# Maxima and denominators by way of DRAM, exp four steps behind, and another rule for handing out the pieces: a stack of four cross-attention layers

## Chip, cores and metric

The kernel runs on one core of a Trainium2 chip. The metric is the device time of one execution in microseconds (us); the time before is the median of three runs, 5645.32 us. The engines are named as the profile names them: PE is TensorE (PEld its weight loads), DVE is VectorE, ACT is ScalarE, POOL is GpSimd, SP is SyncE, whose queue issues most DMAs.

## What is computed

Four cross-attention layers one after another on x of 2048 rows by 256, with a context of 1601 rows by 512 and float32 throughout. Layers 0, 2 and 3 ("masked" in the kernel) have 16 heads of 64; a few columns of the logits get a bias of -20 where a mask says so. Layer 1 ("grouped") normalizes x first and has 16 heads of 16 that share 4 key heads. Cut to what matters:

```python
def masked_layer(h, ctx, Wq, Wk, Wv, Wo, bo, ...):
    q, k, v = h @ Wq, ctx @ Wk, ctx @ Wv                     # 16 heads of 64
    logits = einsum('bhqd,bhkd->bhqk', q, k) * 64 ** -0.5
    logits = logits + col_bias                               # -20 in up to four token columns
    out = einsum('bhqk,bhkd->bhqd', softmax(logits), v)
    return h + out @ Wo + bo

def grouped_layer(x, ctx, wq, wk, wv, wo, norm_w):
    q = rmsnorm(x, norm_w) @ wq                              # 16 heads of 16, 4 key heads
    attn = softmax(einsum('btgrd,bsgd->bgrts', q, ctx @ wk) * 0.25)
    return x + einsum('bgrts,bsgd->btgrd', attn, ctx @ wv) @ wo
```

The softmax is computed with its true row maxima, in two passes over the scores.

## The kernel before

**Blocks, units, steps.** A block is a pair of heads in a masked layer (8 blocks of 4 units: four groups of 512 query rows), or one key head with its four query heads in the grouped layer (4 blocks of 8 units: four groups of rows by two pairs of heads). That makes 128 units, 96 masked and 32 grouped. A unit works with two heads and 512 rows; its 1601 keys are cut into `NT` = 13 chunks of 128 (the last has 65). The main loop at the end of the function runs over steps. In one step TensorE computes the scores of chunk `ca` of unit `ka`, and the exp of another chunk `cb` and the product with the values of a third, `cv`, both of the unit before or the one before that, are done: exp follows the scores by 13 + `DELAY` steps and the values follow exp by `LAG` = 1. "Step 4" of a unit means `ca` = 4 below.

**A masked unit.** Scores go to a PSUM tile `s` (two buffers of two banks each). ACT copies them to SBUF as `p` (L763; a pool `probs` of `NP` = 17 buffers), DVE keeps the running maximum `top` over the chunks (L766, L768). After the last chunk, at step 0 of the next unit, `maxima` turns `top` by eight transposes (L805) and reduces it to `ntop`, the negated maximum of each query row (L806). At step 1 `maxima_spread` brings these values to all partitions with eight more transposes (L818) into the PSUM tile `less`. From step 2 on, DVE adds `less` to `p` (L834), ACT takes exp (L841), and POOL adds the chunks up in `sums` (L844 adds the first two, L846 each further one). TensorE multiplies by the values into `po` (L869), and ACT copies the result to `oT` (L875).

**The end of a unit** goes by pieces: `denominators` turns `sums` by eight transposes (L888), reduces them to one denominator per row (L889) and takes the reciprocal; POOL spreads the two columns over 64 rows each (`by`, L899); `divide` turns `by` with four transposes (L907) and DVE multiplies it with `oT` (L911); `project` multiplies by `Wo` (L917, two pieces) and DVE adds the result to `xs`, the running x (L923). A grouped unit has its denominators as a row of `oT` (L894) and then goes the same way; its scores are computed twice, once for the maxima and once, with the maxima subtracted inside TensorE, for exp.

**The queue of pieces.** What is neither scores nor values is handed out in pieces, mostly one at the end of a step: two query pieces for the next unit (five or three in the grouped layer, with the stacking of split operands), the pieces that end a unit, and the projections of the next block's keys (13 pieces) and values (13). They come in groups; a group that has begun is finished first, then groups in `urgent` go before those in `fill`. `Pieces.step(share)` adds a share to a credit and runs one piece for each whole credit. The share is at least 1, and steps 0 and 1 of a masked unit get none. At step 0 of each unit, before its scores, `flush` runs the group that has begun and everything urgent. Nearly all pieces (not the masked denominators) use the one-bank PSUM tile `pm`, which has one buffer.

**Order.** A loop at the end of the program ties the instructions of TensorE, ACT and DVE to the order in which they are written. POOL's and SP's are ordered by the framework's scheduler.

**Loads.** The transposed context lies in DRAM (`ctxT`); slices of it (`ct`, three buffers) are loaded when the group before the one that uses them begins. `wk` and `wv` have two buffers.

## Time and profile before

| | |
|---|---|
| runs | 5645.32 us median of 3 (5644.31 to 5645.62) |
| profiled execution | 5653.54 us, of it 5651.8 in the span of the profile |
| busy | PE 94%, DVE 71%, ACT 57%, POOL 50% of the span |
| mean granted TensorE clock | 0.980 |
| stages | masked layer 0 to about 1534 us, grouped layer to about 2829, masked layers 2 and 3 to the end |
| PE busy, 170 to 1000 us | 793.79 of 830.00 |
| PE busy, 1534 to 2829 us | 1250.58 of 1295.00 |
| PE busy, 4241 to 5390 us | 1104.34 of 1149.00 |
| costliest group of PE | L869 `po<-p,v`: 1821.7 us |
| costliest group of POOL | L846 `sums<-sums,p`: 2499.2 us, 2367 ns each |
| HBM | 235.27 MB read, 13.76 MB written |

The profile is one execution. "Busy" of PE counts matmuls whose ends are modelled and which are pipelined, so two that follow each other overlap a little in its rows; what one costs is better read from the start of one to the start of the next. In a row such as "PE s L751 <- DVE top L768: 116.4, 71, 2.7" the engine, tile and line that waited stand first, then what it waited for, the total in us, the number of times and the longest. A granted clock of 0.5 means that TensorE got half its pulses.

### The profile page before, as it was taken

How to read it: one execution, taken by the hardware profiler on the slowest of the kernel's cores; microseconds unless marked ns; L12 is line 12 of the kernel's file. 1: busy time of each engine (PE TensorE's matmuls, PEld its weight loads, DVE VectorE, ACT ScalarE, POOL GpSimd, SP SyncE). 2: the span in 40 equal slices, each digit the busy share in tenths (PEclk: the TensorE clock that was granted, in tenths of full speed). 3: DMA queues.
4: the chain of work that ended last, by engine and by line, in shares of the span. 5: the costliest groups of instructions: out<-in, count | busy, mean ns of one | idle time of the engine just before them, and what ended most of it. 6: DMA issues, size and time to landing. Idle time of an engine off the chain costs nothing.

```text
span 5651.8 us, 59516 instructions
## 1 busy us (share of the span) xinstructions
PE 5321.4 (94%) x22444; PEld 1865.2 (33%) x22444; DVE 4013.6 (71%) x4140; ACT 3196.2 (57%) x3513; POOL 2837.7 (50%) x1380
## 2 busy tenths in 40 slices
PE   6999999998889999999999999999999999999997
PEld 3333333332323333233233333333333333333332
DVE  3777777777765555555567777777777777777786
ACT  2666666665433434333456666666666666666665
POOL 1766666665410000000056666666666666666676
PEclk8999999999889999999999999999999999999998
DMA  4112211111100000001012111212111121111100
GB/s 135 32 57 60 59 49 53 55 56 44 39 20 5 9 9 9 9 13 52 15 51 61 56 54 49 57 56 59 46 56 55 54 59 49 53 56 52 54 17 15
DMA packets 209744, 252.88 MB, mean 45 GB/s; under 512 B 43529, under 2 KB 155401, under 8 KB 209456
## 3 DMA queue, kind: packets, MB, share of 16 engines
q1 hardware_dynamic: 206192, 243.69, 14.8%
q8 instruction: 177, 2.90, 0.2%
q0 software_dynamic: 1152, 3.28, 0.2%
q10 hardware_dynamic: 2112, 2.10, 0.1%
q14 instruction: 111, 0.91, 0.1%
HBM read 235.27 MB, written 13.76 MB: 44 GB/s over the span
## 4 chain that ended last, share of the span: by engine, by line
PE 78%; ACT 7%; POOL 7%; DVE 5%; issue 2%; DMA 0%; SPq 0%; ACTq 0%; POOLq 0%; DVEq 0%
PE po L869 24%; PE s L751 20%; PE pm L384 6%; PE pm L369 5%; PE pm L917 5%; POOL sums L844 4%; ACT p L763 4%; ACT p L841 3%; POOL sums L846 3%; PE s L850 2%; PE s L784 2%; PE pm L420 2%; PE s L805 2%; PE b L818 2%; PE s L855 2%
## 5 line engine op out<-in xcount | busy, mean ns | idle before, releaser
L846 POOL TENSOR_TENSOR sums<-sums,p 128x1024 f32<-128x1024 f32 (+1 forms) x1056 | 2499.2, 2367 | 1097.9 <-ACT p L841 1084.8
L763 ACT COPY p<-s 128x1024 f32<-128x1024 f32 (+1 forms) x1248 | 1263.4, 1012 | 1434.0 <-PE s L751 1138.3
L869 PE MATMUL po<-p,v 128*64 128x512 f32 (+1 forms) x6656 | 1821.7, 626 | 36.5 <-ACT p L841 34.7
L768 DVE TENSOR_TENSOR top<-s,top 128x1024 f32<-128x1024 f32 (+1 forms) x1056 | 1291.5, 1223 | 753.9 <-ACT p L763 749.4
L751 PE MATMUL s<-q,kT 64*128 64x512 f32 (+1 forms) x4992 | 1426.3, 648 | 117.6 <-DVE top L768 116.4
L834 DVE TENSOR_TENSOR p<-p,b 128x1024 f32<-128x1024 f32 (+1 forms) x1248 | 1504.7, 1206 | 2.4 <-PE b L818 2.0
L841 ACT ACTIVATE p<-p 128x1024 f32<-128x1024 f32 (+1 forms) x1248 | 1321.5, 1059 | 110.3 <-DVE p L834 109.4
L869 PEld LDWEIGHTS po<-p,v 128*64 128x64 f32 (+1 forms) x6656 | 332.0, 136 | 1032.1 <-issue 698.9
L899 POOL COPY by<-rden 128x512 f32<-128x512 f32 x128 | 78.5, 613 | 1111.8 <-DVE rden L897 1083.9
L751 PEld LDWEIGHTS s<-q,kT 64*128 64x128 f32 (+1 forms) x4992 | 370.7, 182 | 732.7 <-issue 454.6
L859 ACT ACTIVATE p<-s 128x1024 f32<-128x1024 f32 (+1 forms) x283 | 289.8, 1024 | 451.0 <-PE s L855 450.9
L844 POOL TENSOR_TENSOR sums<-p 128x1024 f32<-128x1024 f32 x96 | 226.5, 2360 | 434.2 <-ACT p L841 434.2
L789 DVE TENSOR_REDUCE row_top<-s 128x2 f32<-128x1024 f32 x261 | 318.6, 1221 | 122.9 <-PE s L784 121.9
L384 PEld LDWEIGHTS pm<-wv,ct 128*128 128x128 f32 (+1 forms) x2392 | 284.7, 187 | 218.9 <-issue 215.9
L384 PE MATMUL pm<-wv,ct 128*128 128x128 f32 (+1 forms) x2392 | 337.6, 286 | 0.5 <-ACT v L389 0.5
L369 PE MATMUL pm<-ct,wk 128*128 128x512 f32 (+1 forms) x736 | 315.8, 544 | 2.7 <-ACT kT L374 2.7
L917 PE MATMUL pm<-o,wo 128*128 128x512 f32 x512 | 292.0, 653 | 7.1 <-DVE xs L923 2.9
L859 ACT ACTIVATE p<-b 128x1024 f32<-128x1024 f32 (+1 forms) x133 | 136.2, 1024 | 217.8 <-PE b L855 217.8
L923 DVE TENSOR_TENSOR xs<-pm,xs 128x512 f32<-128x512 f32 x232 | 158.4, 683 | 90.4 <-PE pm L917 90.4
L806 DVE TENSOR_REDUCE ntop<-s 128x8 f32<-128x1024 f32 x96 | 117.6, 1225 | 130.9 <-PE s L805 130.6
L789 DVE TENSOR_REDUCE row_top<-b 128x2 f32<-128x1024 f32 x123 | 150.2, 1221 | 62.2 <-PE b L784 61.6
L420 PE MATMUL pm<-xT,wq 128*128 128x512 f32 x336 | 188.5, 644 | 0.0
(191 smaller groups left out, 3279.2 us busy)
## 6 DMA issues: line engine op xcount, KB each, us to landing
ct<-ctxT SPq DMA_DIRECT2D x288, 512.0 KB, 3.8
xT<-xT SPq DMA_DIRECT2D x104, 512.0 KB, 3.5
ct<-ctxT SPq DMA_DIRECT2D x48, 130.0 KB, 2.6
wk<-in_L_xattn_Wk_dram SPq DMA_DIRECT2D x24, 256.0 KB, 4.4
wv<-in_L_xattn_Wv_dram SPq DMA_DIRECT2D x24, 256.0 KB, 3.1
xT<-xs SPq DMA_DIRECT2D x12, 512.0 KB, 2.6
wq<-in_L_xattn_Wq_dram SPq DMA_DIRECT2D x24, 128.0 KB, 2.1
wo<-in_L_xattn_Wo_dram SPq DMA_DIRECT2D x24, 128.0 KB, 2.1
```

Of the source, the lines that this page charges most:

```text
L369: nc.tensor.matmul(u.pk[:, :n], u.wk[:, k, :], ct(k, a, n), start=(k == 0), stop=(k == NCT - 1),)
L384: nc.tensor.matmul(u.pv[:m, c - c0, :], ct(k, a, m), u.wv[:, k, :], start=(k == 0), stop=(k == NCT - 1),)
L751: nc.tensor.matmul(s[:m, h, :], self.u.kT[r, a : a + m], self.q[r, :], start=True, stop=(a != TAIL),)
L763: nc.scalar.copy(p[:m], s[:m])
L768: nc.vector.tensor_tensor(self.top[:m], s[:m], self.top[:m], ALU.max)
L789: nc.vector.tensor_reduce(self.top[:, :, q, k : k + 1], s, AX.X, ALU.max)
L834: nc.vector.tensor_tensor(self.p[c][:m], self.p[c][:m], self.less[:m], ALU.add)
L841: nc.scalar.activation(p[:m], p[:m], AF.Exp)
L844: nc.gpsimd.tensor_tensor(self.sums, self.p[0], p, ALU.add)
L846: nc.gpsimd.tensor_tensor(self.sums[:m], self.sums[:m], p[:m], ALU.add)
L869: nc.tensor.matmul(self.po[r, :], u.v[:m, c, r], self.p[c][:m, h, :], start=(c == 0), stop=(c == NT - 1),)
L917: nc.tensor.matmul(py, wo[:, ts(k, P)], self.o, start=True, stop=True)
```

## The change

- **Maxima.** `maxima` writes `ntop` to DRAM (1024 values, four at a time) and reads it back into an SBUF tile `spread` on all 128 partitions (512 KB moved), both by SP's queue; `maxima_spread`, now at step 3, is one ACT copy from `spread` into the PSUM tile `less`. L818's transposes go. `DELAY` is 4, and `probs` has 19 buffers.
- **Denominators.** They are taken one head at a time (four transposes into `pm`, a reduce), each counted as half a piece; the reciprocals go the same way by DRAM to a tile `by`, and POOL multiplies `oT` with it in place. L899, L907 and L911 go.
- **Sums.** POOL begins `sums` with a copy of the first chunk.
- **Queue.** A piece returns its cost (1.0 if it returns nothing; `divide`, `keep`, `squares` and the four divisions of `normalize` 0.0). The credit carries at most 0.9 over; the share is what is left divided by the steps left, without a floor of 1, with 5 pieces planned for each further unit of the block. Only step 0 after a masked unit gets none. Queries become due at step 3, denominators at step 6, divide and project at step 11.
- **Loads.** Each `ct` load is issued after the piece that last read the buffer, three at the start of a block. `wk` and `wv` have one buffer.

The diff's core:

```diff
...
     masked_names = ["L0_xattn_", "L2_xattn_", "L3_xattn_"]
-    NP = 17
+    NP = 19
     const = ctx.enter_context(tc.tile_pool(name="const", bufs=1))
...
             u.kT = u.v = None
             u.wq = weights.tile([P, NC, P], FP, name="wq")
-            u.wk = weights.tile([P, NCT, P], FP, name="wk")
-            u.wv = weights.tile([P, NCT, P], FP, name="wv")
+            u.wk = weights.tile([P, NCT, P], FP, name="wk", bufs=1)
+            u.wv = weights.tile([P, NCT, P], FP, name="wv", bufs=1)
             for to, w in ((u.wq, "Wq"), (u.wk, "Wk"), (u.wv, "Wv")):
...
             )
+    def on_all_partitions(cols, to):
+        rows = dram.tile([2, P, QT], FP, name="cols", bufs=4)
+        with nc.allow_non_contiguous_dma(reason="1024 values, four at a time"):
+            nc.sync.dma_start(out=rows.rearrange("h p q -> p h q"), in_=cols)
+        for tile_, heads_ in to:
+            src = rows[heads_].rearrange("(o h) p q -> o (h p q)", o=1)
+            nc.sync.dma_start(out=tile_, in_=src.to_broadcast(tile_.shape))
...
                         nc.tensor.transpose(pt[:, h, q, :], self.top[:, h, ts(q, P)], ident)
                 nc.vector.tensor_reduce(ntop, pt, AX.X, ALU.max, negate=True)
+                self.spread = work.tile([P, 2, P, QT], FP, name="spread", bufs=1)
+                on_all_partitions(
+                    ntop, [(self.spread.rearrange("n h p q -> n (h p q)"), slice(0, 2))]
+                )
             else:
...
             if self.masked:
                 self.less = ps_b.tile([P, 2, QB], FP, name="b")
-                for h in range(2):
-                    for q in range(QT):
-                        nc.tensor.transpose(
-                            self.less[:, h, ts(q, P)],
-                            self.ntop[:, h, q : q + 1].to_broadcast((P, P)), ident,
-                        )
+                nc.scalar.copy(
+                    self.less.rearrange("n h (q p) -> n h q p", p=P),
+                    self.spread.rearrange("n h p q -> n h q p"),
+                )
                 return
...
                 p = self.p[c]
                 nc.scalar.activation(p[:m], p[:m], AF.Exp)
-                if c == 1:
+                if c == 0:
                     self.sums = work.tile([P, 2, QB], FP, name="sums")
-                    nc.gpsimd.tensor_tensor(self.sums, self.p[0], p, ALU.add)
-                elif c:
+                    nc.gpsimd.tensor_copy(self.sums, p)
+                else:
                     nc.gpsimd.tensor_tensor(self.sums[:m], self.sums[:m], p[:m], ALU.add)
...
             return self.sub == len(self.layer.SUBS) - 1
-        def denominators(self):
-            rden = self.rden = small.tile([P, 2, QT], FP, name="rden")
+        def denominators(self, h):
+            if h == 0:
+                self.rden = small.tile([P, 2, QT], FP, name="rden")
+            rden = self.rden
             if self.masked:
-                pt = ps_s.tile([P, 2, QT, P], FP, name="s")
-                for h in range(2):
-                    for q in range(QT):
-                        nc.tensor.transpose(pt[:, h, q, :], self.sums[:, h, ts(q, P)], ident)
-                nc.vector.tensor_reduce(rden, pt, AX.X, ALU.add)
+                pt = ps_m.tile([P, QT, P], FP, name="pm")
+                for q in range(QT):
+                    nc.tensor.transpose(pt[:, q, :], self.sums[:, h, ts(q, P)], ident)
+                nc.vector.tensor_reduce(rden[:, h, :], pt, AX.X, ALU.add)
+                if h == 0:
+                    return 0.5
                 nc.vector.reciprocal(rden, rden)
...
                     )
                 nc.vector.reciprocal(rden, pd.rearrange("p q h -> p h q"))
-            self.by = work.tile([P, QT, 2, 64], FP, name="by", bufs=1)
-            nc.gpsimd.tensor_copy(
-                self.by,
-                rden.rearrange("p h (q o) -> p q h o", o=1).to_broadcast((P, QT, 2, 64)),
+            by = work.tile([P, P, QT], FP, name="by", bufs=1)
+            on_all_partitions(
+                rden,
+                [(by[self.rows(h)].rearrange("r p q -> r (p q)"), slice(h, h + 1)) for h in range(2)],
             )
+            self.by = by.rearrange("r p q -> r q p")
+            return 0.5 if self.masked else 1.0
+        def denominator_groups(self):
+            return [[lambda h=h: self.denominators(h)] for h in range(2 if self.masked else 1)]
         def divide(self):
-            pr = ps_m.tile([P, QB], FP, name="pm")
-            for q in range(QT):
-                nc.tensor.transpose(
-                    pr[:, ts(q, P)], self.by[:, q].rearrange("p h o -> p (h o)"), ident
-                )
-            self.o = work.tile([P, QB], FP, name="o", bufs=1)
-            nc.vector.tensor_tensor(self.o, pr, self.oT, ALU.mult)
+            oT = self.oT.rearrange("r (q p) -> r q p", p=P)
+            nc.gpsimd.tensor_tensor(oT, oT, self.by, ALU.mult)
+            return 0.0
         def project(self, k):
             py = ps_m.tile([P, QB], FP, name="pm")
             wo = self.layer.wo(self.u, self.sub)
-            nc.tensor.matmul(py, wo[:, ts(k, P)], self.o, start=True, stop=True)
+            nc.tensor.matmul(py, wo[:, ts(k, P)], self.oT, start=True, stop=True)
             to = xs[:, self.b, k, :]
...
         def finish_groups(self):
-            return [[self.denominators], [self.divide]] + [
-                [lambda k=k: self.project(k)] for k in range(NC)
-            ]
+            return [[self.divide]] + [[lambda k=k: self.project(k)] for k in range(NC)]
...
                 queue = self.urgent or self.fill
                 if not queue:
-                    return
+                    return 1.0
                 self.now.extend(queue.popleft())
-            self.now.popleft()()
+            cost = self.now.popleft()()
+            return 1.0 if cost is None else cost
         def step(self, share):
-            self.credit = min(self.credit + share, 2.0)
+            self.credit = min(self.credit, 0.9) + share
             while self.credit >= 1.0:
-                self.pop()
-                self.credit -= 1.0
+                self.credit -= self.pop()
...
         layer = layers[l]
         nxt = made[l, n] = layer.load(n)
-        slices = {}
-        ahead = deque()
-        def load(name):
-            if name in ahead:
-                ahead.remove(name)
-                kind, c, a, width = name
-                slices[kind, c] = context_slice(a, width)
+        slices, loads = {}, deque()
         def with_loads(queue):
             found = []
             for name, group in queue:
                 if name:
-                    ahead.append(name)
-                def head(name=name, piece=group[0]):
-                    load(name)
-                    if name and ahead:
-                        load(ahead[0])
-                    piece()
-                found.append([head, *group[1:]])
+                    kind, c, a, width = name
+                    slices[kind, c], tiles = context_slice(a, width)
+                    loads.extend(tiles)
+                    each = len(group) // len(tiles)
+                    def read(j, piece, each=each):
+                        piece()
+                        if (j + 1) % each == 0 and loads:
+                            loads.popleft()()
+                    group = [lambda j=j, piece=piece, r=read: r(j, piece) for j, piece in enumerate(group)]
+                found.append(list(group))
             return found
         first, second = map(with_loads, layer.key_groups(nxt, slices))
+        for _ in range(min(3, len(loads))):
+            loads.popleft()()
...
         return normalize(l + 1, b)
-    DELAY, LAG = 2, 1
+    DELAY, LAG = 4, 1
     N = len(units) * NT
+    due = {}
     turn = 0
-    for step in range(N + NT + DELAY + LAG):
+    for step in range(N + NT + DELAY + LAG + 10):
         ka, ca = divmod(step, NT)
...
                 pieces.flush(pieces.fill, pieces.later)
                 start_block(i)
+        top = of[ka - 1] if 0 < ka <= len(units) and ca < DELAY else None
         three = not (scoring and scoring.masked) and not (exping and exping.masked)
...
         if valuing:
             valuing.values(cv)
-        if top and ca == 1:
+        if top and ca == DELAY - 1:
             top.maxima_spread()
         if scoring and ca == 2 and ka + 1 < len(units):
             ahead = unit_of(ka + 1)
-            pieces.urgent.extend(ahead.layer.unit_groups(ahead))
+            due.setdefault(step + 1, []).extend(ahead.layer.unit_groups(ahead))
         if valuing and cv == NT - 1:
-            pieces.urgent.extend(valuing.finish_groups())
-            pieces.urgent.extend(after(kv))
+            due.setdefault(step + 2, []).extend(valuing.denominator_groups())
+            due.setdefault(step + 7, []).extend(valuing.finish_groups() + after(kv))
+        pieces.urgent.extend(due.pop(step, ()))
         if scoring and ca == 4 and units[ka - 1][:1] == units[ka][:1] != units[ka - 2][:1]:
             pieces.fill.extend(pieces.later)
             pieces.later.clear()
-        if scoring and not (top and top.masked):
+        if scoring and not (top and top.masked and ca == 0):
             i, b, sub = units[ka]
             after_this = sum(u[0] == i for u in units[ka + 1 : ka + 8])
-            steps = NT - ca + (NT - 2) * after_this
-            pieces.step(max(1.0, (pieces.left() + 6 * after_this) / steps))
+            steps = NT - ca + (NT - 1) * after_this
+            pieces.step((pieces.left() + 5 * after_this) / steps)
         elif not scoring:
...
```

More of the change, by code (lines that the diff above doesn't have):

```diff
@@ L200, in context_slice, with load @@
         step = NCT if n <= 256 else NCT // 2
-        tiles = []
-        for k in range(0, NCT, step):
-            ct = work.tile([P, step, 2 * QB // step], FP, name="ct", bufs=3)
+        tiles = {}
+        def load(k):
+            tiles[k] = ct = work.tile([P, step, 2 * QB // step], FP, name="ct", bufs=3)
             nc.sync.dma_start(out=ct[:, :, :n], in_=ctxT_dram[:, k : k + step, a : a + n])
-            tiles.append(ct)
-        return lambda k, b, m: tiles[k // step][:, k % step, b - a : b - a + m]
+        loads = [lambda k=k: load(k) for k in range(0, NCT, step)]
+        return lambda k, b, m: tiles[k - k % step][:, k % step, b - a : b - a + m], loads
     def first_context_slice(i):
@@ L482, in load @@
                         nc.gpsimd.tensor_copy(self.last_k[:, g, to], ident[:, j : j + 16])
-                self.wk = weights.tile([P, NCT, 2, 64], FP, name="wk")
-                self.wv = weights.tile([P, NCT, 64], FP, name="wv")
+                self.wk = weights.tile([P, NCT, 2, 64], FP, name="wk", bufs=1)
+                self.wv = weights.tile([P, NCT, 64], FP, name="wv", bufs=1)
                 for half in range(2):
@@ L674, in squares @@
             nc.scalar.activation(held["x"], xs[:, b], AF.Square)
+            return 0.0
         def rms():
@@ L696, in divide @@
                 nc.sync.dma_start(out=xT_dram[l][b], in_=held["x"])
+            return 0.0
         return [[squares], [rms], *([lambda q=q: divide(q)] for q in range(QT))]
@@ L897, in denominators @@
                 nc.vector.reciprocal(rden, pd.rearrange("p q h -> p h q"))
-            self.by = work.tile([P, QT, 2, 64], FP, name="by", bufs=1)
-            nc.gpsimd.tensor_copy(
-                self.by,
-                rden.rearrange("p h (q o) -> p q h o", o=1).to_broadcast((P, QT, 2, 64)),
-            )
+            by = work.tile([P, P, QT], FP, name="by", bufs=1)
+            on_all_partitions(
+                rden,
+                [(by[self.rows(h)].rearrange("r p q -> r (p q)"), slice(h, h + 1)) for h in range(2)],
+            )
+            self.by = by.rearrange("r p q -> r q p")
+            return 0.5 if self.masked else 1.0
+        def denominator_groups(self):
+            return [[lambda h=h: self.denominators(h)] for h in range(2 if self.masked else 1)]
         def divide(self):
-            pr = ps_m.tile([P, QB], FP, name="pm")
-            for q in range(QT):
-                nc.tensor.transpose(
-                    pr[:, ts(q, P)], self.by[:, q].rearrange("p h o -> p (h o)"), ident
-                )
-            self.o = work.tile([P, QB], FP, name="o", bufs=1)
-            nc.vector.tensor_tensor(self.o, pr, self.oT, ALU.mult)
+            oT = self.oT.rearrange("r (q p) -> r q p", p=P)
+            nc.gpsimd.tensor_tensor(oT, oT, self.by, ALU.mult)
+            return 0.0
         def project(self, k):
@@ L1087, in spare @@
             return ps_s.tile([P, 2, QB], FP, name="s")
-        top = of[ka - 1] if ka and ca < 2 and ka - 1 < len(units) else None
         if step == 3:
```

## The prediction

> **What bounds the kernel now.** I read the busy row first, then the waits of TensorE, then the timeline of one quiet stretch of the masked layers, then two places where the timeline is not quiet.
>
> ```profile
> PE 5321.4 (94%) x22444; PEld 1865.2 (33%) x22444; DVE 4013.6 (71%) x4140; ACT 3196.2 (57%) x3513; POOL 2837.7 (50%) x1380
> ```
>
> The timeline's columns are start, duration, engine, line, operation, tiles; in brackets the idle time before it and its releaser.
>
> ```profile
> 3528.58 1.13 PE L751 MATMUL s<-q,kT 64*128 64x512 f32 x4
> ...
> 3529.64 1.08 PE L869 MATMUL po<-p,v 128*64 128x512 f32 x4
> ...
> 3530.65 1.12 PE L369 MATMUL pm<-ct,wk 128*128 128x512 f32 x2
> ...
> 3530.86 1.22 DVE L768 TENSOR_TENSOR top<-s,top 128x1024 f32<-128x1024 f32 x1 [0.77 <-ACT p L763]
> ...
> 3531.71 1.13 PE L751 MATMUL s<-q,kT 64*128 64x512 f32 x4
> ```
>
> A step is scores 1.06, values 1.01, one queue piece 1.06 (start to start): 3.13 us of TensorE without a hole. Per step ACT has 1.01+1.06, DVE 1.21+1.22, POOL 2.37. So TensorE sets the pace: work taken from it is won, and any hole in it is lost. Its present holes:
>
> ```profile
> PE s L751 <- DVE top L768: 116.4, 71, 2.7
> PE pm L907 <- POOL by L899: 55.9, 79, 4.4
> ```
>
> The first starts at ACT's copy L763 of step 4, which waits for POOL's first sum L844 to free a probability buffer. Grouped layer: 1250.6 us of TensorE in the 1295 us from 1534 to 2829, a step without a piece taking 2.30 (2118.03 to 2120.33). It is TensorE's too.
>
> **What is removed.** L818: eight transposes, 1.02 a unit in the chain of waits, 96 masked units: 98 us. L907: four, 0.55 start to start, 128 units: 70. The hole at L751: POOL's copy frees the first buffer after about 1.2 (twice the 0.61 of the 128x512 copy L899) instead of after the second exp and 2.36, and 19 buffers with four steps' delay leave the same two steps: 116. Next in line there is step 4's exp, a whole step ahead of its values. The hole at L907: 56. Sum 340. DVE loses L911 (88 us) and gains some 17 by two reduces of 0.7 for one of 1.22; it had room, so nothing.
>
> **Maxima by DRAM.** Seen from the start of scores at step 0, ntop is ready at 3.4 (3499.84 to 3503.26). The DMAs: a write of 4 KB in 16-byte pieces, then a 512 KB broadcast in 4 KB rows.
>
> ```profile
> xT<-xT SPq DMA_DIRECT2D x104, 512.0 KB, 3.5
> ...
> wq<-in_L_xattn_Wq_dram SPq DMA_DIRECT2D x24, 128.0 KB, 2.1
> ...
> wo<-in_L_xattn_wo_dram SPq DMA_DIRECT2D x16, 16.0 KB, 1.7
> ...
> tok_idx<-ttn_token_indices_A_dram SPq DMA_DIRECT2D x3, 1.0 KB, 3.2
> ```
>
> The write lies between 1.7 (near in amount) and 3.2 (near in piece size); I take 2.2. The broadcast is like xT, 3.5. It lands at 9.2, at worst 10.3; ACT wants it 3.3 into step 3, at 11.6 to 12.6. Hidden, with 1.3 us left; each us past that costs up to 96. SP holds weights, context and xT loads too, but the trace shows them issued out of written order (wq at 3424.97, its wv at 3500.50), so I let none stand in front. ACT's copy is 96 times about 1.01 (L763), beside TensorE where step 3 has a piece. Where it has none, ACT has 5.7 us for two steps of 5.2, and the next values wait for exp and the oT copy: about 1.0, in half the units: 48.
> The Trainium skill, "DMA: Bandwidth & Descriptors" (Specifications), says that transfers under 512 B are read and rewritten, which speaks against 16-byte writes. No row here prices such a write; the bounds above do without it.
>
> **The queue.** This decides. I stepped the new rule through all steps (share, cost, due step). Pieces that follow each other with no scores between them share the one ps_m bank, and TensorE must wait for the evacuation, which DVE does after that step's maximum. The old kernel has such a pair once:
>
> ```profile
> 2847.64 1.12 PE L917 MATMUL pm<-o,wo 128*128 128x512 f32 x2
> ...
> 2849.46 0.68 DVE L923 TENSOR_TENSOR xs<-pm,xs 128x512 f32<-128x512 f32 x1
> ...
> 2850.19 1.12 PE L917 MATMUL pm<-o,wo 128*128 128x512 f32 x2 [1.43 <-DVE xs L923]
> ```
>
> New pairs in masked units: (a) project(0) and project(1), due at step 11, come together there, or the second is flushed at step 0 just after the first: 86 times. In the quiet frame project ends at 3.13, the maximum at 3.50, the evacuation at 4.2: 1.1 each, 95 us. (b) Both halves of the denominators in one step, since after the first 0.5 the credit is still over 1 (example: shares 0.95, credit 1.58): 64 times. Transposes end at 2.58, reduce at 4.2: 1.67 each, 107. About 30 stand apart and cost DVE's lag, 0.5 each: 15. (c) A last key piece flushed ahead of project waits 0.7 for ACT: 21 times, 15. (d) Steps without a piece wait about 0.1 for exp, one a unit: 10. With ACT's 48: 290.
>
> In grouped blocks the rule plans 5 a unit where about 7 come (queries 3 or 5, denominators 1, projections 2) and key pieces besides. Example, the second grouped block's second unit: 14 pieces left over 82 steps plus 5 for each of 6 units gives a share of 0.54; the five query pieces, due at step 3, take until step 11, and the denominators are left for the flush at step 0, where divide and project follow them at once. TensorE then stands for the whole round trip: DVE 0.6, write 2.2 with its issue, second broadcast 0.4 + 2.1 (wq's row), POOL's multiply 1.2 (half of 2.37): 6.5. In 11 units nothing lies between: 72. In 4, one step of 2.3: 4.2 each, 17. In 14, two steps: 1.9 each, 27. Some 30 pairs of project with project or a stack wait 0.85 (2112.57 to 2113.38): 26. Sum 142.
>
> A hole also slows what follows:
>
> ```profile
> 1478.12 0.58 PE L529 MATMUL pm<-q,sel_qa 128*128 128x512 bf16 x1 [2.61 <-DVE q L536]
> ...
> 1478.64 2.31 PE L751 MATMUL s<-q,kT 64*128 64x512 f32 x4
> ```
>
> Scores took 2.31, not 1.13; the window 1474 to 1482 has a granted clock of 0.79. In the quiet frame 3.4 us at half rate lose 1.7. I give that to the 15 long holes and a third of it to the 14 short: 35. The holes of 1.7 in masked units were there before (71 at L751), so nothing for them.
> The Trainium skill, "TensorE: Matmul & The Clock Gate" (What's actually happening), has half rate follow only an idle window of about 3.4 us. The 2.61 here is less and slowed it all the same; by the rule alone, with nothing for the 14 short holes, the sum would be 9 lower.
>
> **Rest.** Between layers the normalize pieces, spaced a step apart before, come in one bunch in three units (cost 0.0 each): four reciprocals (0.95) with two products (0.61) hold DVE 8.7 us in one go. Between 0 and 50; I take 25. The last block has few pieces, and divide comes one or two steps after the denominators; with the final round trip through DRAM: 15. Single wk and wv buffers cost nothing: wk's last reader is half a block before its next use, and wv is loaded while keys are projected; context loads stay three tiles ahead. If that cover failed, one load of 3.1 to 4.4 a block would show, 28 blocks, 120.
>
> POOL gains 128 multiplies of 1.2 and loses 128 copies of 0.61: about 31 of 40 us a unit. Divide needs no written place on POOL: three to five steps pass between denominators and project in masked units, and POOL waits 0.76 a step.
>
> Sum on the profiled execution's own 5653.5 (span 5651.8 and 1.7 around it): -340 +290 +142 +35 +25 +15 = 5820. The median is 8 below the profiled one: 5812. Between 5645 and this stand 167 us.
>
> **Rivals.** Faster: pairs don't meet. If the evacuation of the first of a pair is done earlier than my frame has it, or the credit spaces them, the 202 us of (a) and (b) are not paid: 5610. It decides once 167 of the 507 us added fail to come. For it: TensorE alone would have 40.1 us a masked unit (busy 166.8 of the 174.0 from 3545 to 3719, four units, less 1.57 each) against 43.5 now. Against: the 1.43 shown, a plain consequence of one bank.
> Slower, divide on POOL stands behind that step's sum: in the frame the sum runs from 3.34 to 5.71 and divide to 6.9, with project waiting since 2.07: 4.8 in 96 units: 6270; half of it, 6040. For it: before, L907 does wait for POOL 79 times. Against: POOL is free between sums.
> Slower, the broadcast lands 2 us late: ACT stops, 96 x 2: 6000. Against: xT's worst landing of 5.2 still comes within 0.5 us.
> The change doesn't free the buffer, the L751 hole staying: 5930.
>
> **Numbers.** Forecast 0.63, pairs apart 0.22 (a tenth of it within 0.2% of no change), POOL order 0.06, late broadcast 0.05, buffer 0.04. Low 5600 leaves out half of that rival, high 5960 the POOL case and part of the late one: under 0.2 together. The forecast's own range is 5700 to 5900: the bunch 0 to 50, the write 1.7 to 3.2, pairs 0.8 to 1.7. About 0.2% (11 us) is what a measurement can tell from no change: faster 0.2, same 0.02, slower 0.78.
>
> **What would show it.** Right: no L818 or L907; the L751 wait for DVE's top nearly gone; TensorE at project waiting for xs and for POOL's divide, some 70 us of the latter in 1534 to 2829; the second half of the denominators waiting for rden; grouped units about 45 us for 40; masked units 43 to 44; more half-clock windows in the grouped layer. Wrong: masked units near 41, grouped units at or below 40, or ACT's less copy waiting on a DMA.

## The result and the profile after

The changed kernel takes 5969.71 us (median of four runs, 5964.33 to 5977.5) against 5644.82 of the kernel before beside it: ratio 1.0577, interval 1.0559 to 1.0596. It is slower, as forecast, but by 325 us instead of 167, 10 us above the range of 5600 to 5960. The profiled execution has a span of 5964.1, 312.3 longer than before. From here on line numbers are those of each kernel's own file; in the changed kernel scores are L766, values L886, project L938.

The busy row of the page shows TensorE 67 us less busy and a lower share of a longer span: the loss is holes and, as shown below, slower matmuls behind them, not added work.

```profile
PE 5254.2 (88%) x21064; PEld 1731.4 (29%) x21164; DVE 3947.2 (66%) x4108; ACT 3370.5 (57%) x3609; POOL 3053.7 (51%) x1476
```

The waits of TensorE name the holes (total us, times, longest):

```profile
PE pm L938 <- POOL oT L931: 209.1, 52, 9.2
PE po L886 <- ACT oT L892: 117.3, 94, 4.1
PE pm L906 <- DVE rden L907: 91.0, 64, 1.6
PE pm L938 <- DVE xs L944: 87.2, 100, 3.5
PE po L886 <- ACT p L858: 40.4, 28, 8.1
PE pm L938 <- ACT kT L376: 16.1, 21, 0.8
```

The 116.4 of scores waiting for the running maximum is gone. Two rows stand here with the forecast's very counts, 64 meetings of the two halves of the denominators and 21 of a key piece with project; the meetings at `xs` on this row are 100: 81 in masked units, where 86 were forecast, and 19 in the grouped layer, where some 30 were. The two largest rows are larger than forecast.

Cut at the maxima of the same units, the two profiled executions differ by stage like this. The last column puts the prediction's terms in the same stages: what is removed shared out by units, the 290 on the 86 units, 142 and 35 on the grouped layer, 25 on the transition, 15 on the end.

| stage | before | after | difference | forecast |
|---|---|---|---|---|
| start | 130.0 | 117.7 | -12.3 | 0 |
| masked, 86 units | 3774.4 | 3823.7 | +49.3 | +14 |
| to the grouped layer | 233.7 | 225.5 | -8.2 | +12 |
| grouped, 32 units and the first masked one behind them | 1294.3 | 1537.8 | +243.5 | +146 |
| last block and tail | 219.4 | 259.3 | +39.9 | -4 |
| sum | 5651.8 | 5964.1 | +312.2 | +168 |

The grouped layer alone holds two thirds of the miss (97 of 144). The window view gives it in one line (window, length, then busy us and count of PE, PEld, DVE, ACT, POOL, the granted clock, DMA share, GB/s):

```profile
1539.00:3077.00 1538.00, 1296.40 (x5285) 394.97 (x5385) 741.51 (x1015) 521.12 (x557) 100.14 (x75) 0.91 0.07 19
```

Before, it was 1250.58 busy of 1295.00 at a clock of 0.98. TensorE now has 250 instructions less there (no L907 transposes), and still 46 us more busy time: its matmuls run at a slower clock, 0.91. The rest are holes. One of its holes, in the timeline of all engines:

```profile
2065.43 1.05 PE L914 MATMUL pm<-den_rows,oT 128*128 128x2 f32 x8
...
2066.52 0.21 DVE L917 RECIPROCAL rden<-pm 128x8 f32<-128x8 f32 x1 [1.52 <-PE pm L914]
2066.76 0.38 SPq L728 DMA_DIRECT2D cols<-rden  x1
...
2069.46 1.09 SPq L731 DMA_DIRECT2D by<-cols  x2
2069.74 1.08 PE L886 MATMUL po<-p,v 128*64 128x512 f32 x4
2073.07 1.52 POOL L931 TENSOR_TENSOR oT<-oT,by 128x512 f32<-128x512 f32 x1 [36.87 <-DMA by<-cols]
2074.64 1.73 PE L938 MATMUL pm<-oT,wo 128*128 128x512 f32 x2 [3.82 <-POOL oT L931]
...
2077.15 2.08 PE L938 MATMUL pm<-oT,wo 128*128 128x512 f32 x2 [0.78 <-DVE xs L944]
```

The lines show the whole round trip: denominators done at 2066.48, reciprocal to 2066.73, the write landed and the broadcasts issued at 2069.46 (2.7), both landed at 2073.07 (3.6), POOL's product done at 2074.59 (1.5): 8.1 us, where the prediction had 6.5. Two steps of scores and values cover the first part; the rest is a hole of 3.82. Then project takes 1.73 and 2.08 instead of 1.13.

### The profile page after: what moved, and what is told of

Read it like the earlier page. It is cut to its first block, busy times and chain, and to the rows that moved or that the text cites. A ratio compares the mean times of both kernels' runs of the same rounds, so it can differ in the third digit from the quotient of the medians.

```text
span 5964.1 us, 58189 instructions
## 1 busy us (share of the span) xinstructions
PE 5254.2 (88%) x21064; PEld 1731.4 (29%) x21164; DVE 3947.2 (66%) x4108; ACT 3370.5 (57%) x3609; POOL 3053.7 (51%) x1476
## 4 chain that ended last, share of the span: by engine, by line
PE 64%; ACT 13%; DVE 11%; DMA 5%; issue 4%; POOL 2%; SPq 0%; ACTq 0%; POOLq 0%; DVEq 0%
PE po L886 19%; PE s L766 16%; ACT p L778 5%; PE pm L938 5%; PE pm L386 4%; PE pm L371 4%; DVE p L851 3%; ACT p L858 3%; DVE top L783 3%; ACT b L835 3%; PE pm L422 3%; DMA by<-cols 2%; PE s L867 2%; PE s L799 2%; PE s L820 2%
## 5 line engine op out<-in xcount | busy, mean ns | idle before, releaser
L863 POOL TENSOR_TENSOR sums<-sums,p 128x1024 f32<-128x1024 f32 (+1 forms) x1152 | 2726.5, 2367 | 1117.8 <-ACT p L858 1067.1
L886 PE MATMUL po<-p,v 128*64 128x512 f32 (+1 forms) x6656 | 1827.6, 628 | 167.0 <-ACT oT L892 117.3
L766 PE MATMUL s<-q,kT 64*128 64x512 f32 (+1 forms) x4992 | 1420.6, 645 | 6.4 <-DVE top L783 3.1
L931 POOL TENSOR_TENSOR oT<-oT,by 128x512 f32<-128x512 f32 x128 | 197.2, 1540 | 1403.5 <-DMA by<-cols 1394.5
L886 PEld LDWEIGHTS po<-p,v 128*64 128x64 f32 (+1 forms) x6656 | 334.0, 136 | 1173.9 <-issue 501.8
L938 PE MATMUL pm<-oT,wo 128*128 128x512 f32 x512 | 335.8, 742 | 321.7 <-POOL oT L931 209.1
L766 PEld LDWEIGHTS s<-q,kT 64*128 64x128 f32 (+1 forms) x4992 | 370.9, 182 | 695.1 <-issue 382.2
L371 PE MATMUL pm<-ct,wk 128*128 128x512 f32 (+1 forms) x736 | 330.0, 552 | 0.9 <-DMA wk<-in_L_xattn_Wk_dram 0.9
L938 PEld LDWEIGHTS pm<-oT,wo 128*128 128x128 f32 x512 | 86.4, 212 | 542.2 <-POOL oT L931 267.3
L861 POOL COPY sums<-p 128x1024 f32<-128x1024 f32 x96 | 99.5, 1036 | 247.8 <-ACT p L858 247.8
L906 PE MATMUL pm<-ident,sums 128*128 128x128 f32 x768 | 127.4, 289 | 94.9 <-DVE rden L907 91.0
```

Of the source, the lines that this page charges most:

```text
L371: nc.tensor.matmul(u.pk[:, :n], u.wk[:, k, :], ct(k, a, n), start=(k == 0), stop=(k == NCT - 1),)
L766: nc.tensor.matmul(s[:m, h, :], self.u.kT[r, a : a + m], self.q[r, :], start=True, stop=(a != TAIL),)
L863: nc.gpsimd.tensor_tensor(self.sums[:m], self.sums[:m], p[:m], ALU.add)
L886: nc.tensor.matmul(self.po[r, :], u.v[:m, c, r], self.p[c][:m, h, :], start=(c == 0), stop=(c == NT - 1),)
L938: nc.tensor.matmul(py, wo[:, ts(k, P)], self.oT, start=True, stop=True)
```

## The experiments

All were timed in three rounds (e11 in one), beside the kernel before, whose median lay between 5642.65 and 5653.92 on the chips used; small differences are therefore taken from the ratios. "Masked unit" is the mean over the 59 units of layers 2 and 3: 44.13 us before, 44.54 after.

**e1, the floor back in the grouped layer.** Is it the even sharing alone that costs the grouped layer its time?

```diff
-            pieces.step((pieces.left() + 5 * after_this) / steps)
+            share = (pieces.left() + 5 * after_this) / steps
+            pieces.step(share if scoring.masked else max(1.0, share))
```

> The changed kernel with one line more: in the grouped layer the share has its floor of 1 back, so the denominators are taken at about step 6 to 9 and divide at step 11 finds its factors landed. Theory (the queue rule makes TensorE stand for the round trip through DRAM, and the half clock follows): the 161.7 us that project waits for POOL's multiply in the grouped layer fall under 30, the half-clock time there from 280 us to under 80, and the time from 5970 to 5740-5790. Rival (the round trip costs by itself, DMAs and strided copies, wherever it stands): above 5900.

Measured: 5708.67, ratio 1.0114 (1.0097 to 1.0131), below what was expected; the grouped layer falls from 1537.8 to 1285.4, less than before the change. Project's wait for POOL falls to 9.6 us in the grouped layer. The same work of TensorE, at the same count, is 75.5 us shorter:

```profile
1533.00:2819.00 1286.00, 1220.89 (x5284) 377.44 (x5385) 737.53 (x1015) 521.61 (x558) 100.97 (x75) 0.98 0.08 23
```

So of the 252 us that one line brings back, 75.5 is clock (1296.40 - 1220.89), 152 the wait for POOL's product (161.7 - 9.6), 10 the wait for `xs`. With pieces in between, the round trip by DRAM is thus nearly hidden: 9.6 us of waiting in the whole grouped layer.

**e2, the old spreading of the denominators in the grouped layer, with the new sharing.** L899, L907 and L911 as before, there alone.

```diff
+            if not self.masked:
+                self.by = work.tile([P, QT, 2, 64], FP, name="by", bufs=1)
+                nc.gpsimd.tensor_copy(self.by, ...)
...
+                    nc.tensor.transpose(pr[:, ts(q, P)], self.by[:, q]..., ident)
+                nc.vector.tensor_tensor(self.oT, pr, self.oT, ALU.mult)
```

> The changed kernel with the old way of spreading the denominators (POOL copy, four transposes, DVE multiply) in the grouped units alone; the queue rule stays. Theory: the denominators are still flushed just ahead of project, but the way from one to the other is about 3 us instead of 8, so the holes shrink to a third and most of the half clock goes: 5780-5840. Rival (it is the bunching of pieces in the one PSUM bank, not the trip): above 5900.

Measured: 5836.14, ratio 1.0348 (1.0331 to 1.0366), grouped layer 1408.0. The short road (POOL, four transposes, DVE) halves the loss but keeps the pieces in a row. Neither the sharing nor the road by DRAM is the cause alone; the sharing that leaves nothing between costs 114 us with the short road (1408.0 against the 1294.3 of the kernel before, which has the floor and the short road) and 252 with the long one (1537.8 against e1's 1285.4).

**e3, DRAM rows in the order of the queries,** so that ACT's copy and POOL's product read without a stride; the write then goes in pieces of 4 bytes.

```diff
-        rows = dram.tile([2, P, QT], FP, name="cols", bufs=4)
+        rows = dram.tile([2, QT, P], FP, name="cols", bufs=4)
...
-            nc.sync.dma_start(out=rows.rearrange("h p q -> p h q"), in_=cols)
+            nc.sync.dma_start(out=rows.rearrange("h q p -> p h q"), in_=cols)
```

> The changed kernel with the values laid out in DRAM as rows of 128 (the write goes in 4-byte pieces instead of 16), so that ACT's copy and POOL's multiply read without a stride. Theory (the stride makes ACT's copy 2.02 instead of 1.01 us, and the values at step 5 wait for the oT copy behind it, 117 us in all): the copy falls to about 1.0, POOL's multiply from 1.54 to 1.2, the wait for oT under 60, and the time by 50 to 110 us, to 5860-5920. Rival (ACT is not in the way; or the 4-byte write takes the gain back by landing later): 5950 or more.

Measured: 7678.58, ratio 1.3606. The copy and the product did become as short as expected (1016 and 1261 ns), but the write of the same 4 KB lands five times later, at about 10 us (DMA issues; last column median us to landing):

```profile
cols<-rden SPq DMA_DIRECT2D x128, 4.0 KB, 10.0
cols<-ntop SPq DMA_DIRECT2D x96, 4.0 KB, 9.8
```

The changed kernel has 2.0 and 2.2 there. Everything hidden before now shows: ACT's copy waits 563.9 us for the broadcast, project 945.2 for POOL.

**e4, the kernel before with POOL's sums begun by a copy,** nothing else.

```diff
-                if c == 1:
+                if c == 0:
...
-                    nc.gpsimd.tensor_tensor(self.sums, self.p[0], p, ALU.add)
-                elif c:
+                    nc.gpsimd.tensor_copy(self.sums, p)
+                else:
```

> The kernel before with one part of the change alone: POOL begins the sums with a copy of the first chunk. Theory (the hole at the scores of step 5, 116 us, is ACT waiting for a probability buffer that the first sum holds): the hole goes and the time falls by 90 to 130 us, to 5515-5555. Rival (another wait, for the denominators' PSUM buffer or DVE, is late at the same place): less than 40 us, 5605 or more.

Measured: 5532.09, ratio 0.9806 (0.979 to 0.9823). Three lines of the change are worth 110 us on their own. The hole that the prediction named shrinks by 86, from 116.4 to:

```profile
PE s L751 <- DVE top L768: 30.5, 71, 2.7
```

Most of the rest is clock. In the masked units (131 to 1385 and 2829 to 5432 us before, 124 to 1342 and 2788 to 5318 here) the same matmuls keep TensorE busy for 3654.1 us instead of 3686.9, 33 less, and the granted clock goes from 0.99 to 1.00: the holes had slowed matmuls too.

**e5, DVE adds the maxima straight from SBUF** (e1 without ACT's copy):

```diff
-                self.less = ps_b.tile([P, 2, QB], FP, name="b")
-                nc.scalar.copy(...)
...
+                    less = self.spread[:m, h].rearrange("n p q -> n q p")
+                    nc.vector.tensor_tensor(p, p, less, ALU.add)
```

> e1 (floor of 1 in the grouped layer) without ACT's copy: DVE adds the maxima straight from the SBUF tile, two buffers of it, one head at a time and through the stride. Theory (ACT's strided copy of 2.02 us pushes the oT copy back and the values of step 5 wait for it): the 118 us wait for oT goes and the time falls by 70 to 120 us from 5709, to 5590-5640, if DVE's two halves take the 1.21 us that one instruction takes now. Rival (the stride costs DVE as much as ACT): 13 x 1 us more on DVE a unit make it the bound, and the time rises above 6000.

Measured: 7638.82, ratio 1.3519: the rival's time. With both operands in SBUF and the stride DVE takes 1.71 us in the mean for each half of a chunk, and POOL's sums take 3.27 instead of 2.37 (groups: count, busy us, mean ns, then the idle time before them):

```profile
L849 DVE TENSOR_TENSOR p<-p,spread 128x512 f32<-128x512 f32 x2304 | 3833.2, 1707 | 4.8 <-DMA spread<-cols 4.7
...
L861 POOL TENSOR_TENSOR sums<-sums,p 128x1024 f32<-128x1024 f32 x1056 | 3452.5, 3269 | 1795.4 <-ACT p L856 1709.9 <-ACT v L391 21.6 <-ACT kT L376 21.3
```

**e8, the same on e4** (maxima by DRAM, no ACT copy, exp four steps behind, old queue and denominators):

> From the other side: e4 (the kernel before with the sums begun by a copy) with the maxima by DRAM added straight from SBUF, exp four steps behind, 19 buffers, pieces in step 1 too, the denominators in the PSUM tile that less no longer needs; the old queue rule, the old division. Theory (TensorE's eight transposes L818, 98 us in all, are a gain once nothing waits for what replaces them): 5400-5470 from 5532. Rival (DVE pays for the stride or the two instructions): above 5700.

Measured: 7593.78, ratio 1.3451: DVE's half is 1.82, POOL's sum 3.21. With the old queue rule it is as slow, so the new rule is not the cause.

**e11, e5 with the stride taken out.** `spread` is read in its own order, so the maxima go to the wrong queries; the amount of work is that of e5.

> As the kernel in which DVE adds the maxima straight from SBUF (7639), but it reads them without the stride of 16 bytes, so they are added in the wrong order; the amount of work is the same. Theory: DVE's 1.74 a half and POOL's slower sums come from two operands in SBUF, whatever the stride: DVE 1.6 to 1.75 a half, 7300 to 7640. Rival: the stride is what costs: DVE falls to about 0.68 a half as with PSUM, POOL's sums back to about 2.4, and the time to 5570 to 5640.

Measured: 7225.7, ratio 1.2779. DVE 1.47 a half, POOL's sum 2.62:

```profile
L849 DVE TENSOR_TENSOR p<-p,spread 128x512 f32<-128x512 f32 x2304 | 3293.0, 1468 | 5.0 <-POOL sums L861 2.5 <-DMA spread<-cols 2.3
...
L861 POOL TENSOR_TENSOR sums<-sums,p 128x1024 f32<-128x1024 f32 x1056 | 2766.8, 2620 | 2240.4 <-ACT p L856 2215.2 <-DMA by<-cols 10.2 <-ACT kT L376 6.5
```

It lies a little below the theory's numbers and far from the rival's: of the 1.03 us that a half has gained over the 0.68 read from PSUM (e7), 0.79 stays without the stride. But these are means, and the trace shows that the second SBUF operand costs nothing by itself. The 471 of the 2496 adds during which POOL runs nothing take 0.64 to 0.69 us, no more than with one operand in PSUM; of the other 2025, 865 are as short, and the longer ones, up to 2.89, all have a POOL instruction beside them. Two adds while POOL is idle, then two beside its sum:

```profile
4043.93 1.28 DVE L849 TENSOR_TENSOR p<-p,spread 128x512 f32<-128x512 f32 x2
...
4047.43 3.44 DVE L849 TENSOR_TENSOR p<-p,spread 128x512 f32<-128x512 f32 x2
4047.44 2.88 POOL L861 TENSOR_TENSOR sums<-sums,p 128x1024 f32<-128x1024 f32 x1 [7.19 <-ACT p L856]
```

With one operand in PSUM the adds stay at 0.63 to 0.69 beside POOL too (e7). The stride has a price of its own: in e5 the 381 adds that run while POOL is idle take 1.07 in the mean, for 0.68. So what makes e5, e8 and e11 slow is above all DVE's adds and POOL's sums in each other's way, and the stride comes on top.

**e6, the masked denominators as one piece** of eight transposes in a scores tile (on e1):

```diff
-                pt = ps_m.tile([P, QT, P], FP, name="pm")
+                pt = ps_s.tile([P, 2, QT, P], FP, name="s")
...
-            return 0.5 if self.masked else 1.0
+            return 1.0
```

> e1 with the masked denominators as one piece of eight transposes in a two-bank buffer of the scores, as before the change. Theory (the second half waits for the reduce of the first in the one pm bank, 93 us in all): that wait goes, and of it 50 to 95 us come off, 5615-5660. Rival (the buffer of the scores is as scarce; the scores wait instead): less than 25 us, 5685 or more.

Measured: 5630.28, ratio 0.9979 (0.9968 to 0.9989), 78 us below e1. The row of `rden` (93.2 in e1) is gone; a new one, scores for `top`, is 38.9.

**e7, ACT's copy without a stride** (on e1): the broadcast is copied as it lies, and DVE reads PSUM across the stride, a head at a time.

```diff
-                    self.less.rearrange("n h (q p) -> n h q p", p=P),
-                    self.spread.rearrange("n h p q -> n h q p"),
+                    self.less.rearrange("n h f -> n (h f)"),
+                    self.spread.rearrange("n h p q -> n (h p q)"),
...
+                    less = self.less[:m, h, :].rearrange("n (p q) -> n q p", q=QT)
+                    nc.vector.tensor_tensor(p, p, less, ALU.add)
```

> e1 with ACT's copy unstrided on both sides and the stride moved to DVE's reading of the PSUM tile, one head at a time. Theory: ACT's copy falls from 2.02 to about 1.0 and the wait for oT from 118 us to under 50; if DVE reads PSUM with a stride at its usual rate the time is 5630-5670. Rival (DVE pays for the stride): DVE's 1.21 us become 2 or more and the time rises above 6000.

Measured: 5625.78, ratio 0.9969 (0.9958 to 0.9981), 83 us below e1. The copy falls from 2023 ns to 1006, and the values' wait for ACT's `oT` from 118.0 to:

```profile
PE po L889 <- ACT oT L895: 39.6, 51, 3.2
```

DVE's two halves read from PSUM across the stride cost 676 ns each, 1.35 for the 1.21 of the one instruction.

**e9, e6 and e7 together:**

> The changed kernel with the floor of the share back in the grouped layer, the denominators as one piece of eight transposes in a scores tile, and ACT's copy of the maxima unstrided (DVE reads the PSUM tile across its stride). If the two masked costs are separate holes, their gains add: 5709 - 78 - 83 = 5548, masked units at 44.65 - 0.83 - 0.95 = 42.9 us, and the hole at project for xs stays at about 65 to 90 us as the largest. Rival: both shorten the same stretch of the unit (steps 3 to 6), the second gain is mostly covered by the first: 5610 to 5630.

Measured: 5553.67, ratio 0.9821 (0.9805 to 0.9838); masked units 42.96. The sum of the two was 1.0114 - 0.0135 - 0.0145 = 0.9834: they add, so the two holes are separate. The wait for `xs` at project is the largest left (80.6).

**e12, e9 with the floor of 1 everywhere:**

```diff
-            pieces.step(share if scoring.masked else max(1.0, share))
+            pieces.step(max(1.0, share))
```

> The kernel with both masked costs mended (5554), with the floor of 1 on the share in the masked layers and the last block too, not in the grouped layer alone: the pieces are no longer spread evenly anywhere. Theory: a share below 1 is what brings project's two pieces together (81 us of waits for xs) and what leaves the last block's denominators so late that project waits for POOL's product (30 us of its 174 + 73): both go, 5460 to 5500, masked units at 42.1 to 42.4, the last block at 150 to 160. Rival: project's pieces meet because they fall due at step 11 and are flushed two steps later, and the last block waits because it has no other pieces; the share has no part in it: 5540 to 5560.

Measured: 5513.54, ratio 0.9765 (0.9748 to 0.9781), between the two: 32 us below e9 by the ratios. The theory holds for the last block (174.2 to 155.2; from there to the end project waits 11.2 for POOL's product, in two waits, for 30.0 in six); some 17 more, by the two profiles, lie in the start and the first masked layer, which were not expected to move. For project's pairs the rival holds: masked units 42.97, the wait for `xs` 86.4. The timeline at the end of a unit shows why:

```profile
3265.36 1.12 PE L371 MATMUL pm<-ct,wk 128*128 128x512 f32 x2
...
3267.25 1.10 PE L940 MATMUL pm<-oT,wo 128*128 128x512 f32 x2 [0.77 <-ACT kT L376]
...
3269.13 1.12 PE L940 MATMUL pm<-oT,wo 128*128 128x512 f32 x2 [0.79 <-DVE xs L946]
```

Project falls due at step 11, a group of four key pieces has begun and goes first, and both halves are flushed at step 0 behind it. An earlier due step was not tried.

**e10, e4 with the maxima by DRAM,** copied by ACT as in e7, exp four steps behind, 19 buffers, one buffer for `wk` and `wv`; denominators, transposes of `by` and the floor as before; what ends a unit is queued one step later than before:

```diff
+                nc.scalar.copy(
+                    self.less.rearrange("n h f -> n (h f)"),
+                    self.spread.rearrange("n h p q -> n (h p q)"),
+                )
...
-    DELAY, LAG = 2, 1
+    DELAY, LAG = 4, 1
...
-        if scoring and not (top and top.masked):
+        if scoring and not (top and top.masked and ca == 0):
...
-            pieces.urgent.extend(valuing.finish_groups())
-            pieces.urgent.extend(after(kv))
+            late = valuing.finish_groups() + after(kv)
```

> The kernel before with POOL beginning its sums by a copy (5532), and the maxima alone by DRAM: ntop written and broadcast, ACT's copy unstrided into PSUM, exp four steps behind, 19 buffers, one buffer for wk and wv; denominators, L907, the floor of the share and the order of the pieces as before. Theory: the transposes of L818 (98 us) go and nothing takes their place, since ACT's copy of 1.0 lies beside a piece of TensorE: 5430 to 5460, masked units at 41.9. Rival: the copy in ACT's queue holds exp up as in the changed kernel (about 40 us left), and the pieces that now run at steps 1 and 2 meet new evacuations: 5490 to 5540, no gain over the copy alone.

Measured: 5470.07, ratio 0.9675 (0.9659 to 0.9691), the fastest of all. The maxima by DRAM, with all that comes with them in this edit, are worth 0.0131 of 5645, 74 of the 98 us expected; masked units 42.31. Its largest holes:

```profile
PE pm L923 <- POOL by L915: 71.9, 96, 3.4
PE po L885 <- ACT p L857: 39.8, 34, 4.7
PE s L762 <- DVE top L779: 34.5, 83, 2.0
```

## Why the prediction was wrong in size

**What held.** TensorE sets the pace, and the queue's rule decides: with the floor (e1) the kernel is 5709. The hole at the scores went with the freed buffer (3.1 left of 116.4). That e4's 110 lies so near the forecast 116 is partly luck: there the hole shrinks by 86 only, and 33 come from the clock, for which the forecast had nothing in the masked units. The broadcast was in time: its write landed after 2.2 and the 512 KB after 3.8, and ACT waited 3.8 us for it in all. The counts of meetings, stepped by hand through the rule, were 64 of 64 and 21 of 21, and each cost close to what the frame said: the `rden` pairs 1.42 for 1.67, project behind a key piece 0.77 for 0.7; 72 us (87.2 less the 14.9 in the grouped layer) for the 95 of project's pairs. The 32 units whose halves stand apart show no wait at all, where 15 was forecast. None of the rivals came: pairs did meet, POOL had the product done in time in nearly all masked units, and the L751 hole went.

**What failed.** The mechanisms came, but three terms of the sum were too small: the round trip in the grouped layer by 46, the half clock behind it by 40, ACT's copy in the masked units by 69. The pairs, cheaper than forecast (91 for 122 at `rden`, 72 for 95 at `xs`), hid 54 of that.

**The step that failed first: the round trip in the grouped layer (142).** Its count was right, 29 holes forecast and 30 in the trace, but not the 6.5 us of one trip. The second broadcast was priced by `wq`'s 2.1 and lands at 3.2, the write took 2.7 in the hole shown for 2.2, and POOL's product, taken as half of a sum, 1.2, takes 1.54 because it reads `by` with a stride (1.26 without, in e3):

```profile
L931 POOL TENSOR_TENSOR oT<-oT,by 128x512 f32<-128x512 f32 x128 | 197.2, 1540 | 1403.5 <-DMA by<-cols 1394.5
```

With 8.1 in place of 6.5 the same counts give 11 x 8.1 + 4 x 5.8 + 14 x 3.5 = 161; the trace has 161.7 where 116 was forecast. An error of 1.6 us in one trip became 46, since every hole starts where cover ends and takes the whole error. The agreement is not only in the sum: of the 28 trips of grouped units with a hole, the trace has 10 with nothing in between, 4 with one step, 13 with two and 1 with three, and from the denominators' last matmul to project they take 7.3 to 9.2 us (the other two of the 30 holes belong to the last masked units).

**The half clock after the holes (35).** e1 against the changed kernel, with the same matmuls, prices it at 75.5, about 2.5 for each of 30 holes instead of 1.7 and 0.6. The rule of the Trainium skill, "TensorE: Matmul & The Clock Gate" (What's actually happening), that half rate follows an idle window of about 3.4 us, would have made the sum 9 smaller still. This trace has half rate behind shorter holes too: the granted clock is 0.57 from 2750 to 2758, where a hole of 2.94 ends at 2751.6, and from 2795 to 2799, just behind one of 2.75. The hole of 3.82 above is followed by 10 us with a granted clock of 0.91 (2080 to 2090). The prediction charged one window to the long holes and a third to the short.

**ACT's copy (48).** Taken as 1.01 like L763, it takes 2.02, because it reads `spread` with a stride of 16 bytes:

```profile
L835 ACT COPY b<-spread 128x1024 f32<-128x1024 f32 x96 | 194.2, 2023 | 3.8 <-DMA spread<-cols 3.8
```

The chain then is the one that the prediction described, in nearly all units instead of half: the add, exp and `oT` come late, and the next values wait for `oT`.

```profile
3274.86 2.02 ACT L835 COPY b<-spread 128x1024 f32<-128x1024 f32 x1
...
3276.99 1.22 DVE L851 TENSOR_TENSOR p<-p,b 128x1024 f32<-128x1024 f32 x1 [1.72 <-ACT b L835]
...
3279.21 0.57 ACT L892 COPY oT<-po 128x512 f32<-128x512 f32 x1
...
3279.83 1.08 PE L886 MATMUL po<-p,v 128*64 128x512 f32 x4 [1.62 <-ACT oT L892]
```

94 waits, 117 us for 48. e7 takes the stride away and gains 83.

**Smaller terms.** The last block and the tail were given 15, less 19 of work and waits removed, and became 40 longer: with few pieces the share is far below 1, the denominators come late, and project stands in the same round trip (34.9 us there); against before, these two stages are 27.7 longer in e9 and 9.1 in e12. The normalize bunch, given 25, did not show: the transition became 8 shorter. The start, given nothing, differs by 12, but it ranged from 116 to 131 over the kernels with no pattern that the edits explain; its cause is open. So is what the division by DRAM is worth in the masked layers by itself: no run here separates it.

## What to carry to other kernels

Where a chain is only just covered, price every link by a row with the same access pattern, not only the same size: a stride or a smaller piece doubled one link and made another five times as long here, and a link's error is paid in full at every place where the cover ends. Spreading work evenly brought nothing on an engine that is nearly always busy: the kernel that does it nowhere (e12) is 32 us faster than the one that does it in the masked layers (e9). What counts is that something independent stands between two pieces that share a buffer or wait for a round trip. When a change has several parts, time each alone: one part of three lines gained 110 us, and the bundle hid it. And a mean over many instructions can hide two populations: the adds of e11 cost 1.47 us in the mean, but 0.68 wherever POOL was idle.

## What the runs showed of the hardware

- ACT copies 128x1024 float32 from SBUF to PSUM in 1.01 us, and in 2.02 when it reads with a stride of four values (16 bytes). DVE reading PSUM with that stride takes 676 ns for 128x512, with no such loss (e7; its add to `xs`, of the same size and without a stride, takes 688); reading SBUF with it DVE takes 1.07 us for 0.68 while POOL is idle (e5, e11). The Trainium skill, "SBUF — State Buffer" (Door 1: The DMA port swizzle), says that an access that crosses to a new line of 16 bytes pays a penalty, and gives no price; ACT's row agrees.
- A write of 4 KB to DRAM lands at 2.0 to 2.2 us in 16-byte pieces and at 9.8 to 10.0 in 4-byte pieces.
- DVE's add of 128x512 takes 0.68 us with one operand in PSUM, beside POOL or not (e7), and the same with both in SBUF while POOL is idle. Beside POOL's sums the adds with both in SBUF take up to 2.89 (1.47 in the mean over all of them, 1.71 with the stride), and the sums go from 2.37 to 2.62 and 3.27. The same page (Who interferes with whom) says that a DVE instruction with two SBUF inputs contends with a GpSimd instruction that reads SBUF; the trace of e11 agrees, since no add above 0.69 is without a POOL instruction beside it.
- Half rate after holes adds almost half of the holes themselves: 75.5 us of slower matmuls beside 162 us of waiting in the grouped layer.
